# Two 1x1 products of a two-layer attention kernel: from 128 stationary columns at once to two halves of 64

## Chip, cores and metric

The kernel runs on one core of a Trainium2 chip. The metric is the device time of one execution in microseconds (us); lower is better. Times are the median of three runs where nothing else is said. A profile is one further execution, recorded by the hardware profiler.

## The reference, cut to what matters

The input x has 8 images of 256 channels and 96 x 96 pixels, in float32. Two layers follow one another, each with a group norm ahead of it and the input added after it.

```python
# layer 0: attention between channels of the 2-D Fourier transform
q_f, k_f, v_f = (fft2(pconv(gn(x), w, b)) for w, b in ((w1, b1), (w2, b2), (w3, b3)))
attn = einsum('bhcn,bhdn->bhcd', normalize(q_f), normalize(k_f)) * temperature
attn = complex(softmax(attn.real), softmax(attn.imag))
out  = abs(ifft2(einsum('bhcd,bhdn->bhcn', attn, v_f)))
x    = x + pconv(out, w_out)                       # pconv: product over the 256 channels
# layer 1: linear attention with softplus features, over the pixels
x    = x + linear_attention(gn(x), Wq, bq, Wk, bk, Wv, bv)
```

The kernel takes no Fourier transform of the images. It uses that the attention matrix of layer 0 follows from sums over pairs of pixels, and that the inverse transform of the weighted values is a fixed mixing of x with a reversed copy of it.

## The kernel before, in words

**Stages.** For each image there are five. (1) *Gram sums*: the 256 x 256 sums over pixels of products of channels, for the even and the odd part of the image (`pair_sums`, L465, with `products`, L448; image 0 has its own form, `first_sums`, L369). (2) *Attention*: softmax and the small matrices made of it, among them `mz`, the stationary matrix of z (`attention`, L556). (3) *Rotation* of the image into the array y (`rotate`, L752). (4) *Images* (`images`, L827): z = mz x y, then e = the magnitude of z, then the projection of e by `wo`, added to x. (5) *Layer 1* (`layer1`, L932, and `output`, L1120).

**Stage 4 in detail.** The 9216 pixels are cut into 24 chunks (index i) of CH = 384. For each chunk, `apply` (L864) makes two tiles of z, c = 0 and 1, each 128 output channels by 384 pixels, as the sum of two products over k (128 input channels each), at L867. VectorE adds a table and writes e (L912), ScalarE squares (L916), GpSimd adds the two halves of e (L917), ScalarE takes the root (L918, L919). The projection (`project`, L870) of the chunk two places back follows: two tiles m of 128 x 384, each a sum over two k, at L875; VectorE adds them to x (L877) and takes the statistics for the next group norm (L296). At i = 0, 8 and 16 a third, narrow kind of z is made for eight chunks at once ("z16", 32 output channels for each, four of them side by side in the array, also at L867); VectorE reads it at L897. z tiles lie in the PSUM pool `ps` (5 buffers), projection tiles in `acc` (3 buffers) or `ps`.

**Gram sums in detail.** `turn_blocks(u)` (L484) transposes 32 x 32 blocks of the next image on VectorE (L503) and, for every second u, sends the result to DRAM for later use (the transfer xtd, L508) and issues the load of a later group (`load_grouped`, L137, with its DMAs at L153 and L155). `pair(u)` (L512) makes the even and the odd part, eo, on GpSimd (L518, L530) and on GpSimd or VectorE (L531). `products` (L448) then multiplies eo with itself, in one step for each of up to three q: 8 products with 64 stationary columns, which go to the upper and the lower 64 partitions of a PSUM tile by turns (m % 2), at L462. There are 37 steps for an image after the first. eo and e share a ring of five SBUF buffers.

**What sets the order.** The order on each engine is written out by hand: it is the program order within `manual_schedule` (L1202). The stages are Python generators, and `weave` (L1111) advances the Gram sums of the next image by as many steps as a stage yields. `images` yields 1 after chunk 15 (the preparation of Gram's first pair), 2.5 after each of the chunks 16 to 23 (L924), and 1 before each of the two last projections; `layer1` yields too. So from chunk 16 on TensorE gets z, projection, then two or three Gram steps, and so on. Before chunk 16, and in the last image (which has no next one), z and projection follow each other alone. All DMAs are issued from SyncE's queue (SP).

**The lines touched.** `columns` (L743) gives the stationary columns of z:

```python
        return t[:, k, c * P:(c + 1) * P] if c < 2 else t[:, k, 2 * P:2 * P + 32]
```

A step of Gram sums uses half of the columns of the array in each product:

```python
                o = acc[c][m % 2 * HP:m % 2 * HP + HP, to:to + n]
                nc.tensor.matmul(o, lhsT=v[:, 1 + m * HP:1 + (m + 1) * HP], rhs=of, ...)
```

Here P = 128 and HP = 64.

Of the kernel before, what the change touches and what calls it, by code (L numbers as in the profile page):

```python
# [57 lines left out]
P = 128  # L58
HP = 64
KC = 2  # L60
# [14 lines left out]
def two_layer_kernel(ctx: ExitStack, tc: tile.TileContext, x, w1t, b1, w2t, b2, w3, b3, wot, temp,  # L75
                     wqt, bq, wkt, bk, wvt, bv, gavg, gmat, tmat, out):
    nc = tc.nc
# [4 lines left out]
    CH = 384  # L82
    PR = CH // W
# [33 lines left out]
    def ring_tile(name):  # L117
        return ring.tile([P, 2 * NQ * (C + 2)], F32, tag="ring", name=name)

    def ps_tile(name):  # L120
        return psum.tile([P, 512], F32, tag="ps", name=name)

    def load_x(b, t):
        nc.sync.dma_start(out=x_of(b)[:, :, t * TW:(t + 1) * TW], in_=x_v[b, :, :, t * TW:(t + 1) * TW])
# [12 lines left out]
    def load_grouped(b, v):  # L137

        xs = x[b].rearrange("(c i) h w -> i c h w", i=32)
        if 2 * v == NG:  # L140
            m = H // 2
            f, g = (staged(b, v, i)[:, 0:C].rearrange("p (c w) -> p c w", c=NB8) for i in range(2))
            for q in range(NQ):
                s = slice(32 * q, 32 * q + 32)
                n = 32 if q else 31
                o = W + 1 - 32 * (q + 1)
                nc.sync.dma_start(out=f[s], in_=xs[:, :, m, s])
                nc.sync.dma_start(out=g[s, :, 0:n], in_=xs[:, :, m, o:o + n])
            return
        f, g = (staged(b, v, i)[:, 0:SG].rearrange("p (c w) -> p c w", c=NB8) for i in range(2))  # L150
        for a in range(G):
            h, s = 2 * (G * v + a), slice(32 * a, 32 * a + 32)
            nc.sync.dma_start(out=f[s], in_=xs[:, :, h:h + 2].rearrange("p c r w -> p c (r w)"))  # L153
            if h:
                nc.sync.dma_start(out=g[s], in_=xs[:, :, H - h - 1:H - h + 1].rearrange("p c r w -> p c (r w)"))  # L155
            else:
                nc.sync.dma_start(out=g[s, :, 0:W], in_=xs[:, :, H - 1])
                nc.sync.dma_start(out=g[s, :, W:2 * W], in_=xs[:, :, 0])
# [39 lines left out]
    wo = const.tile([P, KC, C], F32, name="wo")  # L198
# [96 lines left out]
    def stats_chunk(st, b, c, k):  # L295
        nc.vector.bn_stats(out=st[:, k, c, :], in_=x_of(b)[:, k, c * CH:(c + 1) * CH])  # L296
# [4 lines left out]
    def aggregate(mv, st, k):  # L301
        nc.vector.bn_aggr(out=mv[:, k, :], in_=st[:, k, :, :].rearrange("p n s -> p (n s)"))  # L302
# [440 lines left out]
    def columns(t, k, c, j):  # L743

        return t[:, k, c * P:(c + 1) * P] if c < 2 else t[:, k, 2 * P:2 * P + 32]

    def blocks(c):
        return [slice(0, P)] if c < 2 else [slice(32 * j, 32 * j + 32) for j in range(4)]
# [78 lines left out]
    def images(b):  # L827
        mz, nmean, beta = m0.pop(b)
# [5 lines left out]
        for c in range(3):  # L834
            for j, r in enumerate(blocks(c)):
                for k in range(KC):
                    nc.tensor.matmul(pg[r, c * (H + 1):(c + 1) * (H + 1)], lhsT=columns(mz, k, c, j), rhs=ys[:, k, :],
                                          start=(c == 0 and k == 0), stop=(k == KC - 1), skip_group_check=True)
# [22 lines left out]
        st1 = new_stats(f"st1_{b}")  # L861
        mv = two.tile([P, KC, 2], F32, tag="mv", name=f"mv_b{b}")

        def apply(out, k, c, j, i):  # L864

            f, o = divmod(PR * i, HB)
            nc.tensor.matmul(out[:, 0:CH].rearrange("p (h q) -> p h q", q=PR), lhsT=columns(mz, k, c, j),  # L867
                             rhs=yz[:, k, f, :, o:o + PR], start=(k == 0), stop=(k == KC - 1), skip_group_check=True)

        def project(i, e):  # L870
            n = slice(i * CH, (i + 1) * CH)
            for m in range(KC):
                po = (ps_tile if m and b + 1 < B and i >= WI - 1 else acc_tile)(f"po_{b}_{i}_{m}")
                for k in range(KC):
                    nc.tensor.matmul(po[:, 0:CH], lhsT=wo[:, k, m * P:(m + 1) * P], rhs=e[:, k, :],  # L875
                                     start=(k == 0), stop=(k == KC - 1))
                nc.vector.tensor_add(x[:, m, n], x[:, m, n], po[:, 0:CH])  # L877
                if i == NC - 1:
                    stats_chunk(st1, b, i, m)
                    aggregate(mv, st1, m)  # L880
            if i < NC - 1:
                for m in range(KC):
                    stats_chunk(st1, b, i, m)

        pending = []
        for i in range(NC):
            if i % 8 == 0:
                v16 = []
                p16 = [ps_tile(f"z16_{b}_{i + t}") for t in (0, 4)]
                for t in range(2):  # L890
                    for k in range(KC):
                        for j, r in enumerate(blocks(2)):
                            apply(p16[t][r], k, 2, j, i + 4 * t + j)
                for t in range(2):
                    v = two.tile([P, CH], F32, tag="v16", name=f"v16_{b}_{i + 4 * t}")
                    v3 = v.rearrange("p (q h) -> p q h", h=H)
                    nc.vector.tensor_add(v3, p16[t][:, 0:CH].rearrange("p (h q) -> p q h", h=H),  # L897
                                         tab16.unsqueeze(1).to_broadcast([P, PR, H]))
                    nc.scalar.activation(v, v, AF.Square)
                    nc.gpsimd.tensor_add(v3, v3, sg[2].unsqueeze(1).to_broadcast([P, PR, H]))  # L900
                    v16.append(v)
            if i % 2 == 0 and 3 + i // 2 < NT:
                for t in range(0 if i == 0 else 3 + i // 2, 4 + i // 2):
                    load_x(b, t)
            if b + 1 < B and i in (12, 13):
                load_grouped(b + 1, i - 12)
            e = ring_tile(f"e_{b}_{i}")[:, 0:4 * CH].rearrange("p (t n) -> p t n", t=4)
            for c in range(2):
                pz = ps_tile(f"z_{b}_{i}_{c}")
                for k in range(KC):  # L910
                    apply(pz, k, c, 0, i)
                nc.vector.tensor_add(  # L912
                    e[:, 2 * c:2 * c + 2, :].rearrange("p t (q h) -> p t q h", h=H),
                    pz[:, 0:CH].rearrange("p (h q) -> p q h", h=H).unsqueeze(1).to_broadcast([P, 2, PR, H]),
                    tab[c].unsqueeze(2).to_broadcast([P, 2, PR, H]))
            nc.scalar.activation(e, e, AF.Square)  # L916
            nc.gpsimd.tensor_add(e[:, 0:2, :], e[:, 0:2, :], e[:, 2:4, :])  # L917
            nc.scalar.activation(e[:, 0:2, :], e[:, 0:2, :], AF.Sqrt)  # L918
            nc.scalar.activation(e[0:NH, 1, :], v16[i % 8 // 4][32 * (i % 4):32 * (i % 4) + NH, :], AF.Sqrt)  # L919
            pending.append((i, e))  # L920
            if len(pending) > 2:
                project(*pending.pop(0))
            if i >= WI:
                yield 2.5 if i > WI else 1  # L924
        for p in pending:
            yield 1
            project(*p)
# [274 lines left out]
    with tc.manual_schedule(engines={E.PE, E.DVE, E.Pool, E.SP, E.Activation}):  # L1202
        sums, loads, parts = first_sums(), first_loads(), tables()
        fetch, turns = rotate(0)
        next(loads)
        next(parts)
        next(loads)
        next(parts)
        next(loads)
        next(parts)  # L1210
        finish(loads)
        for i, _ in enumerate(sums):
            if i > 9:
                next(parts, None)
            if i > 14:
                next(turns)
        finish(mix(0, attention(0), turns))
        for b in range(B):
            sums = pair_sums(b + 1) if b + 1 < B else iter(())
            weave(images(b), sums)  # L1220
            weave(layer1(b), sums)
            if b + 1 < B:
                fetch, turns = rotate(b + 1)
                mixed = mix(b + 1, attention(b + 1), turns)
                output(b, *l1.pop(b), fetch, sums, mixed)
                finish(mixed)
            else:
                output(b, *l1.pop(b))
# [50 lines left out]
```

## Time and profile before

| what | value |
|---|---|
| median of three runs | 2517.08 us (2514.93 to 2518.08) |
| profiled execution, its own time | 2517.73 us |
| its span, first to last instruction | 2515.9 us, 47,106 instructions |
| mean granted TensorE clock | 0.991 |
| L867, z, 128 columns wide: passes, mean of one | 1536, 491 ns |
| L867, z16, 32 columns wide: passes, mean of one | 768, 488 ns |
| L875, projection, 128 columns wide: passes, mean of one | 1536, 488 ns |
| L462, Gram sums, 64 columns wide: passes | 4928 |
| chunks 16 to 23 of one image (849 to 926 us): busy PE, DVE, ACT, POOL | 76.62, 63.53, 23.79, 40.87 us of 77.00 |

How to read it: PE is TensorE's matmul part and PEld its loading of stationary columns; DVE is VectorE, ACT ScalarE, POOL GpSimd, SP the queue that issues DMAs. A group is named by its line, engine, operation and tile, as "L867 PE MATMUL z<-arena,mz 128*128 128x384": z is written from arena (here y) and mz, with 128 rows by 128 columns of the array in use and a moving operand of 128 x 384. A float32 product is recorded as two passes, each with a load of its own; the counts are of passes. Matmuls are pipelined and their ends are modelled, so the mean of one is longer than the distance from one start to the next. "A <- B" in a wait means that A's engine was idle until B; "<- issue" means that the profile shows nothing that was waited for.

### The profile page before, as it was taken

The numbers are of one execution on the slowest core, as the hardware profiler recorded it, in microseconds if no ns is written. First come the engines' busy times: TensorE is split into PE (matmuls) and PEld (weight loads), VectorE is DVE, ScalarE is ACT, GpSimd is POOL, SyncE is SP. The second block draws the span as 40 slices with busy tenths as digits, with TensorE's granted clock in tenths as the row PEclk, the third lists the DMA queues.
The fourth block names the chain that finished last, engine by engine and source line by source line (L and its number), as shares of the span: only waits on it lengthen the run. The fifth ranks groups of instructions, "written<-read, shape, count | busy, mean of one in ns | idle before, by whom it ended". The sixth has DMA issues, their size and how long they took to land. (4 is left out here: it accounts for less than half of the span.)

```text
span 2515.9 us, 47106 instructions
## 1 busy us (share of the span) xinstructions
PE 2475.3 (98%) x18448; PEld 1694.3 (67%) x18448; DVE 1783.9 (71%) x3472; ACT 1164.4 (46%) x2053; POOL 860.4 (34%) x820
## 2 busy tenths in 40 slices
PE   9999999999999999999999999999999999999998
PEld 7875667656686667856668566685666756677546
DVE  4467876687866878578775787757876578866776
ACT  3345364443545445354443535435363453634553
POOL 4124513245123442144331452413524136142311
PEclk9999999999999999999999999999999999999997
DMA  7134729356292653916559263683638627296004
GB/s 229 37 129 100 179 73 324 136 133 179 82 329 91 163 149 123 336 58 161 136 183 318 47 170 96 236 264 63 167 83 295 205 63 198 52 326 200 1 7 151
DMA packets 264665, 394.40 MB, mean 157 GB/s; under 512 B 37400, under 2 KB 194300, under 8 KB 264444
## 3 DMA queue, kind: packets, MB, share of 16 engines
q1 hardware_dynamic: 264444, 391.38, 52.7%
q8 instruction: 147, 2.41, 0.4%
q14 instruction: 74, 0.61, 0.1%
HBM read 246.99 MB, written 144.32 MB: 156 GB/s over the span
## 5 line engine op out<-in xcount | busy, mean ns | idle before, releaser
L867 PE MATMUL z<-arena,mz 128*128 128x384 f32 (+1 forms) x2304 | 596.9, 490 | 0.0
L917 POOL TENSOR_TENSOR e<-e 128x768 f32<-128x768 f32 x192 | 348.6, 1815 | 547.7 <-ACT e L916 521.5
L875 PE MATMUL po<-e,wo 128*128 128x384 f32 x1536 | 529.0, 488 | 1.7 <-ACT e L918 1.7
L867 PEld LDWEIGHTS z<-arena,mz 128*128 128x128 f32 (+1 forms) x2304 | 309.9, 163 | 243.2 <-issue 57.8
L875 PEld LDWEIGHTS po<-e,wo 128*128 128x128 f32 x1536 | 289.9, 190 | 207.1 <-ACT e L918 7.2
L912 DVE TENSOR_TENSOR e<-z,xT 128x768 f32<-128x768 f32 x384 | 360.9, 949 | 61.1 <-PE z L867 59.4
L806 PEld LDWEIGHTS y<-tm,arena 96*128 96x128 f32 x3072 | 360.4, 192 | 36.6 <-issue 24.8
L462 PE MATMUL acc<-eo 128*64 128x193 f32 (+6 forms) x4928 | 381.2, 305 | 0.0
L462 PEld LDWEIGHTS acc<-eo 128*64 128x64 f32 (+1 forms) x4928 | 311.3, 136 | 102.7 <-issue 75.5
L806 PE MATMUL y<-tm,arena 96*128 96x128 f32 x3072 | 380.3, 278 | 0.0
L916 ACT ACTIVATE e<-e 128x1536 f32<-128x1536 f32 x192 | 284.4, 1481 | 166.6 <-DVE e L912 164.3
L918 ACT ACTIVATE e<-e 128x768 f32<-128x768 f32 x192 | 161.9, 843 | 382.0 <-POOL e L917 378.1
L877 DVE TENSOR_TENSOR arena<-arena,po 128x384 f32<-128x384 f32 x384 | 209.1, 550 | 175.1 <-PE po L875 173.8
L530 POOL TENSOR_TENSOR eo<-arena 128x768 f32<-128x768 f32 x77 | 157.3, 2043 | 408.4 <-DVE arena L503 309.2
L1172 POOL TENSOR_TENSOR arena<-arena,po 128x384 f32<-128x384 f32 x180 | 178.6, 1011 | 207.8 <-ACT po L1171 202.4
L812 DVE COPY arena<-y 128x384 f32<-128x384 f32 (+1 forms) x192 | 104.5, 544 | 146.1 <-PE y L806 145.0
L812 ACT COPY arena<-y 128x384 f32<-128x384 f32 (+1 forms) x200 | 94.5, 472 | 231.9 <-PE y L806 214.0
L296 DVE BATCH_NORM_STATS2 st<-arena 128x6 f32<-128x384 f32 x384 | 195.0, 547 | 0.6
L1171 ACT COPY po<-o 128x384 f32<-128x384 f32 x180 | 78.5, 481 | 192.0 <-PE o L1163 189.0
L503 DVE STREAM_TRANSPOSE arena<-arena 128x768 f32<-128x768 f32 x168 | 155.1, 955 | 9.1 <-DMA xtd<-arena 7.2
L1032 PE MATMUL xT<-ident,arena 128*128 128x128 f32 x1152 | 144.1, 275 | 1.3 <-ACT xT L1035 1.3
L1032 PEld LDWEIGHTS xT<-ident,arena 128*128 128x128 f32 x1152 | 127.1, 141 | 19.0 <-issue 16.5
(249 smaller groups left out, 2584.0 us busy)
## 6 DMA issues: line engine op xcount, KB each, us to landing
arena<-in_x_dram SPq DMA_DIRECT2D x106, 768.0 KB
out_dram<-arena SPq DMA_DIRECT2D x192, 384.0 KB
xtd<-arena SPq DMA_DIRECT2D x42, 1536.0 KB
arena<-xtd SPq DMA_DIRECT2D x168, 384.0 KB
arena<-in_x_dram SPq DMA_DIRECT2D x329, 192.0 KB
tm<-rx SPq DMA_DIRECT2D x96, 159.0 KB
wl<-in_w1t_dram SPq DMA_DIRECT2D x8, 256.0 KB
wl<-in_w2t_dram SPq DMA_DIRECT2D x8, 256.0 KB
```

The source lines that it names most:

```text
L296: nc.vector.bn_stats(out=st[:, k, c, :], in_=x_of(b)[:, k, c * CH:(c + 1) * CH])
L462: nc.tensor.matmul(o, lhsT=v[:, 1 + m * HP:1 + (m + 1) * HP], rhs=of, start=(first and m < 2), stop=last, skip_group_check=True)
L806: nc.tensor.matmul(pu[:, o:o + P], lhsT=xt[:, s, k * P:(k + 1) * P], rhs=tm[:, n:n + P], start=True, stop=True)
L812: copy(y[:, :, :, g:g + nr, :], v.rearrange("p k r (f w) -> p k f r w", f=2))
L867: nc.tensor.matmul(out[:, 0:CH].rearrange("p (h q) -> p h q", q=PR), lhsT=columns(mz, k, c, j), rhs=yz[:, k, f, :, o:o + PR], start=(k == ...
L875: nc.tensor.matmul(po[:, 0:CH], lhsT=wo[:, k, m * P:(m + 1) * P], rhs=e[:, k, :], start=(k == 0), stop=(k == KC - 1))
L877: nc.vector.tensor_add(x[:, m, n], x[:, m, n], po[:, 0:CH])
L912: nc.vector.tensor_add(e[:, 2 * c:2 * c + 2, :].rearrange("p t (q h) -> p t q h", h=H), pz[:, 0:CH].rearrange("p (h q) -> p q h", h=H).uns ...
L916: nc.scalar.activation(e, e, AF.Square)
L917: nc.gpsimd.tensor_add(e[:, 0:2, :], e[:, 0:2, :], e[:, 2:4, :])
L1032: nc.tensor.transpose(pt[:, j * C + k * P:j * C + (k + 1) * P], x[:, k, o:o + P], ident)
L1172: nc.gpsimd.tensor_add(x[:, m, r], x[:, m, r], t)
```

## The change

Each z product with 128 stationary columns, and each product of the projection, becomes two with 64: one for output channels 0 to 63, one for 64 to 127, written to the upper and the lower 64 partitions of the same PSUM tile. The moving operand is the same for both. The halves alternate inside the loop over k. The narrow z16 products, everything on other engines, and the order of the stages stay.

```diff
--- before.py
+++ after.py
@@ -861,10 +861,12 @@
         st1 = new_stats(f"st1_{b}")
         mv = two.tile([P, KC, 2], F32, tag="mv", name=f"mv_b{b}")
 
-        def apply(out, k, c, j, i):
+        halves = [slice(HP * h, HP * h + HP) for h in range(2)]
+
+        def apply(out, k, c, j, i, h=slice(None)):
 
             f, o = divmod(PR * i, HB)
-            nc.tensor.matmul(out[:, 0:CH].rearrange("p (h q) -> p h q", q=PR), lhsT=columns(mz, k, c, j),
+            nc.tensor.matmul(out[:, 0:CH].rearrange("p (h q) -> p h q", q=PR), lhsT=columns(mz, k, c, j)[:, h],
                              rhs=yz[:, k, f, :, o:o + PR], start=(k == 0), stop=(k == KC - 1), skip_group_check=True)
 
         def project(i, e):
@@ -872,8 +874,9 @@
             for m in range(KC):
                 po = (ps_tile if m and b + 1 < B and i >= WI - 1 else acc_tile)(f"po_{b}_{i}_{m}")
                 for k in range(KC):
-                    nc.tensor.matmul(po[:, 0:CH], lhsT=wo[:, k, m * P:(m + 1) * P], rhs=e[:, k, :],
-                                     start=(k == 0), stop=(k == KC - 1))
+                    for h in halves:
+                        nc.tensor.matmul(po[h, 0:CH], lhsT=wo[:, k, m * P:(m + 1) * P][:, h], rhs=e[:, k, :],
+                                         start=(k == 0), stop=(k == KC - 1), skip_group_check=True)
                 nc.vector.tensor_add(x[:, m, n], x[:, m, n], po[:, 0:CH])
                 if i == NC - 1:
                     stats_chunk(st1, b, i, m)
@@ -908,7 +911,8 @@
             for c in range(2):
                 pz = ps_tile(f"z_{b}_{i}_{c}")
                 for k in range(KC):
-                    apply(pz, k, c, 0, i)
+                    for h in halves:
+                        apply(pz[h], k, c, 0, i, h)
                 nc.vector.tensor_add(
                     e[:, 2 * c:2 * c + 2, :].rearrange("p t (q h) -> p t q h", h=H),
                     pz[:, 0:CH].rearrange("p (h q) -> p q h", h=H).unsqueeze(1).to_broadcast([P, 2, PR, H]),
```

## The prediction, made before the changed kernel was run

> **What bounds the kernel now.** I read the page's first part, then the groups of instructions with shapes kept apart, then the waits, and last the timeline of the stretches in which the changed products run.
>
> ```profile
> PE 2475.3 (98%) x18448; PEld 1694.3 (67%) x18448; DVE 1783.9 (71%) x3472; ACT 1164.4 (46%) x2053; POOL 860.4 (34%) x820
> ...
> PEld acc L462 <- issue: 75.5, 155, 1.1
> ...
> PEld z L867 <- issue: 57.8, 226, 0.6
> ```
>
> TensorE is busy all the time and in the list of waits it waits for nobody by more than a few us; so its own time is the kernel's time. The two lines on PEld (the weight loads) are the ones that matter: loads of the Gram sums (L462) and of z (L867) come late by "issue", for which the profile shows no releaser. The timeline shows what that is. First, an image's early part, with z and projection only; then the late part, with Gram sums between them (columns: start us, length us, what, number of passes; each fp32 product is recorded as two passes).
>
> ```profile
> 775.42 2.74 PE L867 MATMUL z<-arena,mz 128*128 128x384 f32 x8
> 778.00 2.74 PE L875 MATMUL po<-e,wo 128*128 128x384 f32 x8
> ```
>
> ```profile
> 1182.88 3.51 PE L462 MATMUL acc<-eo 128*64 128x193 f32 x48
> 1186.32 2.85 PE L867 MATMUL z<-arena,mz 128*128 128x384 f32 x8
> 1189.01 2.74 PE L875 MATMUL po<-e,wo 128*128 128x384 f32 x8
> 1191.68 2.42 PE L462 MATMUL acc<-eo 128*64 128x193 f32 x32
> 1194.03 2.85 PE L867 MATMUL z<-arena,mz 128*128 128x384 f32 x8
> ```
>
> Read the starts, not the lengths (ends are modelled). Undisturbed, 8 passes take 778.00 - 775.42 = 2.58, that is 322.5 ns each. In the late part z takes 2.69 (+0.11) and the projection 2.67 (+0.09). Gram takes 3.44 for 48 passes and 2.35 for 32, so 16 passes (one step) take 1.09 to 1.10, and 3.44 - 3 x 1.095 = 0.155 is left over. A round trip from 128 columns to 64 and back thus loses 0.11 + 0.09 + 0.155 = about 0.35 us in which nothing is computed, though no operand is late.
>
> [...] 0.09 to 0.10 on each side of a Gram burst, and nothing between z and projection, which have different operands but one shape. [...] After a drain the first load has no matmul to lie under, and the trace shows it: z's first product is late by 0.11; of Gram's 0.155, some 0.10 is the drain and 0.05 the load. [...] 16 Gram passes are 8 side-by-side pairs of 193 and 130 columns, 2 x (2 x 193 + 2 x 130) = 1292 columns in 1.095 us, 1.18 columns per ns, against 384/322.5 = 1.19 for full width. Four z products of 32 columns (the z16 part) side by side also go at one quad per 0.32 to 0.33:
>
> ```profile
> 763.12 0.15 PEld L867 LDWEIGHTS z<-arena,mz 128*32 128x32 f32 x4 [0.17 <-issue]
> 763.45 0.15 PEld L867 LDWEIGHTS z<-arena,mz 128*32 128x32 f32 x4 [0.17 <-issue]
> 763.77 0.15 PEld L867 LDWEIGHTS z<-arena,mz 128*32 128x32 f32 x4 [0.17 <-issue]
> ```
>
> **The change, part by part.**
>
> *The halves themselves.* 1536 z passes and 1536 projection passes of 128 columns become 3072 pairs of 64. The order (half 0, half 1, then the next k) alternates the two column tiles as Gram's m does, so I expect pairs. Their pace is the unknown. Per pair Gram has 1.095/8 = 137 ns for a mean of 161.5 columns; [...] Bounds: below, no gain (the columns streamed are the same); above, Gram's rate per column, 384/1.18 = 325.5 ns, +3 ns x 3072 = 9.2 us. I take 0 and keep 9.2. The 3072 matmuls and 3072 loads more are 4 instructions per 322.5 ns, 12 per us; Gram runs 32 per 1.095, 29 per us, so issuing hides under the matmuls, and so do two loads of about 0.14 each. If that cover failed it would show as the slower rival below. Readers on VectorE wait for half 1's last pass, some 13 ns later: nothing.
>
> *Drains removed.* By the code, an image with Gram beside it has Gram after i = 16 to 23 (8 bursts) and after each of the two last projections: 10 entries from the projection, of which 9 return to z or projection (the tenth goes to the 128-column group norm and keeps its cost). Seven images have one. An entry loses 0.09 + 0.05 = 0.145 or so, a return 0.10 + 0.11 = 0.205. 70 x 0.145 + 63 x 0.205 = 10.2 + 12.9 = **23.1 us**.
>
> *z16 to z.* 24 switches from 32 columns to 128 become 32 to 64: the drain stays, the open load is half, 24 x 0.053 = **1.3 us**. Projection to z16 keeps its drain.
>
> *Given back at the image's ends.* The group norm after the last burst waits for the mean and variance, which follow the last projection through VectorE (the wait of gm_b for mv_b). So the last entry's 0.145 only lengthens that wait: -7 x 0.145 = -1.0. At an image's start the first projection waits for the first e, so that z16's gain is doubtful: -8 x 0.053 = -0.4. In the last image a new switch 64 to 128 falls into a wait of over 2 us: 0.
>
> *Given back at Gram's operands.* This is the term I am least sure of. TensorE comes earlier to each Gram pair u; does its operand eo? In the third image:
>
> ```profile
> 854.33 0.38 SPq L508 DMA_DIRECT2D xtd<-arena  x1
> 860.92 1.84 DVE L503 STREAM_TRANSPOSE arena<-arena 128x768 f32<-128x768 f32 x2 [0.93 <-DMA xtd<-arena]
> 868.01 2.59 POOL L530 TENSOR_TENSOR eo<-arena 128x768 f32<-128x768 f32 x1
> 870.30 2.42 PE L462 MATMUL acc<-eo 128*64 128x193 f32 x32
> 877.69 1.84 POOL L531 TENSOR_TENSOR eo<-arena 128x768 f32<-128x768 f32 x1
> 878.01 3.51 PE L462 MATMUL acc<-eo 128*64 128x193 f32 x48
> ```
>
> Pair 2 is ready at 868.01 + 2.59 = 870.60 and used at the second step of its burst, 870.30 + 0.05 + 1.10 = 871.45: 0.85 to spare. Pair 3 is ready at 879.53 and used at the third step, 878.01 + 0.05 + 2.20 = 880.26: 0.73 to spare (in the other six images the same rows give 0.45 to 0.77, mean 0.66). From 846 to 874 VectorE runs without waiting for TensorE (transposes, then a wait for the xtd transfer, then e, which GpSimd needs before it starts on eo). So these two times don't move with TensorE. Before pair 3, TensorE will have saved 0.05 + 4 x 0.145 + 3 x 0.205 = 1.25. It therefore waits for 1.25 - 0.66 = 0.59, plus some 0.10 to start again (0.05 from an ACT end to the load it releases, as for the first projection of an image, and the open load of 0.05): 0.69 x 7 = **-4.8 us**. From both sides: 0, if the chain moves along after all; -1.25 x 7 = -8.8 if nothing is to spare. Later pairs have 1.45 and more to spare, with VectorE paced by z again.
>
> **The sum**, against the profiled execution's 2517.73 (span 2515.9 and 1.8 around it): 23.1 + 1.3 - 1.0 - 0.4 - 4.8 = 18.2 us less, 2499.5. That execution is 0.65 above the median of 2517.08, so for the median **2499.0 us** (0.7% less).
>
> **Rivals.**
>
> *A, slower: the two halves don't start together.* In the z16 rows four loads of 0.11 are spread over 0.15, 13 ns from one to the next. If every pair paid such a stagger in the array, 3072 x 13 = 40 us come on top: 2499 + 40 = 2539. For it: two tiles reading the very same moving columns at once is what Gram, with different columns, doesn't show. Against: quads and Gram pairs keep the full pace in spite of their stagger. It decides from 18.2/3072 = 5.9 ns per pair on, and beyond 7.6 ns the kernel is slower by 0.2%.
>
> *B, no change: the gap isn't the tiling.* It could be the semaphore on z's first load, or the change of shape of the moving operand. Then it stays, and the time is 2517, give or take 3. Against: Gram's first load after the projection waits for no semaphore and loses as much; projection after z waits for one and loses nothing.
>
> *C, a smaller gain: pairs at Gram's pace per column (+9.2), or Gram starved by its operands beyond what I took (-4 more):* 2503 to 2511, middle 2508.
>
> **How the numbers follow.** Forecast 0.80, around 2499; its own range goes from 2493 (no give-back at the operands: 2517.1 - 23.0 = 2494, and one more for the spread of the runs, 2514.9 to 2518.1) to 2504. C 0.08, B 0.05, A 0.07. The range of 8 in 10 reaches into C: 2493 to 2508. A difference of under 0.2% (5 us) can't be told from none; forecast and C are faster than that: faster 0.88, same 0.05, slower 0.07.
>
> **What would show it.** Right: z and projection in pairs, 16 passes per 2.58 us in the early part; in the late part 2.58 too, and Gram steps at 1.095 with no rest; PEld's "issue" before L462 and L867 falling from 75.5 and 57.8 to a small part (the z16 switches remain); a new wait of TensorE on POOL eo of some 0.6 us once per image, seven times. Wrong: 16 passes over 2.60 us (A or C), drains that remain at the bursts' edges (B), or waits for eo of over a us. The likeliest error is in the give-back, which is worth up to 5 us either way.

## The result, and the profile after

| | before | after |
|---|---|---|
| median of four runs each | 2516.01 us (2513.68 to 2518.08) | 2494.79 us (2492.63 to 2495.90) |
| ratio, with its 95% interval | | 0.9915 (0.9898 to 0.9932) |
| profiled execution, its span | 2517.73, 2515.9 us | 2492.63, 2490.8 us |

The changed kernel is 21.2 us (0.85%) faster; the prediction said 2499.0, 18.2 us faster. In the lines of the kernel after, z is L869, the projection L878, its add to x L880, the add on VectorE that makes e L916, the sum of e's halves on GpSimd L921; L462, L503, L530 and L531 have kept their numbers. First the busy times, then the lines of the list of waits that answer to those shown of before.

```profile
PE 2446.4 (98%) x21520; PEld 1573.5 (63%) x21520; DVE 1785.9 (72%) x3472; ACT 1163.7 (47%) x2053; POOL 861.9 (35%) x820
```

```profile
PEld z L869 <- issue: 289.4, 1534, 0.6
PEld po L878 <- issue: 237.2, 1353, 0.2
PEld acc L462 <- issue: 54.8, 192, 1.1
...
PEld acc L462 <- POOL eo L530: 1.4, 5, 0.4
```

TensorE still sets the time. PE's busy time fell by 29 us although its passes rose from 18448 to 21520. "issue" ahead of z did not fall but rose fivefold; the last line, a wait for GpSimd's eo, is new and small. Both are taken up below. Now the timeline: the early part of an image, and the late part of the third image with Gram sums between (start us, length us, what, passes).

```profile
772.95 2.75 PE L869 MATMUL z<-arena,mz 128*64 128x384 f32 x16
775.53 2.75 PE L878 MATMUL po<-e,wo 128*64 128x384 f32 x16
```

```profile
853.34 3.47 PE L462 MATMUL acc<-eo 128*64 128x193 f32 x48
856.63 2.76 PE L869 MATMUL z<-arena,mz 128*64 128x384 f32 x16
859.21 2.76 PE L878 MATMUL po<-e,wo 128*64 128x384 f32 x16
861.79 2.48 PE L462 MATMUL acc<-eo 128*64 128x193 f32 x32
```

Twice the passes of half the width take what the full ones took: 775.53 - 772.95 = 2.58. In the late part z and projection now take 2.58 as well (859.21 - 856.63 and 861.79 - 859.21), where 2.69 and 2.67 stood. A burst of 48 Gram passes takes 856.63 - 853.34 = 3.29 = 3 x 1.097 and leaves no rest. After the burst of 32 the next z starts at 864.09; so it takes 2.30, 0.11 more than two steps: that is a wait for pair 2 (kernel 11 below makes it go away).

A single number sums this up for each kernel: the length of the stage, from an image's first pass for the tables that are added to z (tile zs) to the first pass of its group norm (tile gm_b). In the third image that is 760.41 to 925.15 before and 752.88 to 914.33 after: 164.74 and 161.45. The mean over the seven images with Gram sums beside them goes from 164.75 to 161.56, 3.19 each; the last image, which has none, from 137.75 to 137.47. Together 7 x 3.19 + 0.28 = 22.6 us, which accounts for the 21.2 between the medians. The rest of an image (gm_b to the next zs) takes 140.1 to 140.3 in both kernels, but for 0.3 more behind the sixth image in both, and for 1.57 more in some places (twice before, once after); what that is stands at the end. The two profiled executions differ by more than the medians do, 25.1 us in their spans. The 2.5 that are left lie outside the stage: one place of 1.57 less, 0.1 more in each of the seven gaps between images, 1.8 less behind the last group norm and 0.3 more ahead of the first image. Except for the 0.1 per gap, which all kernels with a projection in halves or quarters show, nothing ties them to the change.

### The profile page after: what moved, and what is told of

Same layout as the page of the kernel before. It is cut to its first block, busy times and chain, and to the rows that moved or that the text cites. A ratio compares the mean times of both kernels' runs of the same rounds, so it can differ in the third digit from the quotient of the medians.

```text
span 2490.8 us, 53254 instructions
## 1 busy us (share of the span) xinstructions
PE 2446.4 (98%) x21520; PEld 1573.5 (63%) x21520; DVE 1785.9 (72%) x3472; ACT 1163.7 (47%) x2053; POOL 861.9 (35%) x820
## 5 line engine op out<-in xcount | busy, mean ns | idle before, releaser
L869 PE MATMUL z<-arena,mz 128*64 128x384 f32 (+1 forms) x3840 | 592.4, 487 | 0.0
L921 POOL TENSOR_TENSOR e<-e 128x768 f32<-128x768 f32 x192 | 349.5, 1820 | 533.1 <-ACT e L920 507.1
L878 PE MATMUL po<-e,wo 128*64 128x384 f32 x3072 | 529.5, 486 | 1.8 <-ACT e L922 1.8
L869 PEld LDWEIGHTS z<-arena,mz 128*64 128x64 f32 (+1 forms) x3840 | 245.4, 131 | 296.0 <-issue 289.4
L878 PEld LDWEIGHTS po<-e,wo 128*64 128x64 f32 x3072 | 227.9, 137 | 266.3 <-issue 237.2
L916 DVE TENSOR_TENSOR e<-z,xT 128x768 f32<-128x768 f32 x384 | 358.9, 947 | 43.4 <-PE z L869 42.6
L462 PE MATMUL acc<-eo 128*64 128x193 f32 (+6 forms) x4928 | 379.1, 303 | 1.1 <-DVE eo L417 0.9
L462 PEld LDWEIGHTS acc<-eo 128*64 128x64 f32 (+1 forms) x4928 | 326.5, 136 | 82.0 <-issue 54.8
L880 DVE TENSOR_TENSOR arena<-arena,po 128x384 f32<-128x384 f32 x384 | 208.2, 550 | 153.8 <-PE po L878 153.5
L530 POOL TENSOR_TENSOR eo<-arena 128x768 f32<-128x768 f32 x77 | 157.6, 2047 | 399.7 <-DVE arena L503 309.1
L503 DVE STREAM_TRANSPOSE arena<-arena 128x768 f32<-128x768 f32 x168 | 155.0, 954 | 23.3 <-DMA xtd<-arena 20.5
```

Of the source, the lines that this page charges most:

```text
L878: nc.tensor.matmul(po[h, 0:CH], lhsT=wo[:, k, m * P:(m + 1) * P][:, h], rhs=e[:, k, :], start=(k == 0), stop=(k == KC - 1), skip_group_che ...
L916: nc.vector.tensor_add(e[:, 2 * c:2 * c + 2, :].rearrange("p t (q h) -> p t q h", h=H), pz[:, 0:CH].rearrange("p (h q) -> p q h", h=H).uns ...
```

## The experiments

**Theory.** What went is the loss at each change between 128 and 64 columns; the halves themselves cost nothing; and the Gram sums' operands give back part of it. **Rivals.** The gain comes from something else in the narrower products (one product alone would bring part of it); the pairs have a price that other savings hide; the give-back at the operands is large or nil. No kernel here leaves out or changes any of the computation: edits split products, or move them. "Stage" is the length just defined, and times "against before" are against the kernel before on the same chip (2516.18, one run, for kernels 1 to 4, 2516.81 for 5 to 8, 2514.76 for 9 to 12). Kernels without an interval had one profiled run; such a total can be off by a few us, so the argument rests on the stage and on rows.

### 1. Only z in halves

The projection goes back to one product of 128 columns.

```diff
-                    for h in halves:
-                        nc.tensor.matmul(po[h, 0:CH], lhsT=wo[:, k, m * P:(m + 1) * P][:, h], rhs=e[:, k, :],
-                                         start=(k == 0), stop=(k == KC - 1), skip_group_check=True)
+                    nc.tensor.matmul(po[:, 0:CH], lhsT=wo[:, k, m * P:(m + 1) * P], rhs=e[:, k, :],
+                                     start=(k == 0), stop=(k == KC - 1))
```

> Halves for z alone, the projection in one piece of 128 columns. Theory (what was saved is the switch of tiling, 0.145 us from 128 to 64 columns and 0.205 back): now every chunk has both switches. Per image with Gram beside it, against the kernel before: 22 switches z to projection (+4.5), 12 back to z (+1.7), 7 returns from Gram to z saved (-1.4), z16 to z (-0.2): +4.7 us; last image +7.1. In all +40 us: 2556 against 2516. Rival (the halves save something of their own, or the gap belongs to the Gram operands and not to the tiling): each half of the change brings its share, so 2505 to 2510.

Measured: 2553.99, 38 us slower than before; the stage is longer than before's by 4.46 per image with Gram (4.7 worked out) and by 6.7 in the last one (7.1). Its timeline, in the early part where no Gram sums run (the projection is L877 in this kernel):

```profile
781.37 2.85 PE L877 MATMUL po<-e,wo 128*128 128x384 f32 x8 [0.18 <-ACT e L921]
784.14 2.80 PE L869 MATMUL z<-arena,mz 128*64 128x384 f32 x16
786.88 2.85 PE L877 MATMUL po<-e,wo 128*128 128x384 f32 x8
```

z in halves takes 786.88 - 784.14 = 2.74 and the projection at full width 784.14 - 781.37 = 2.77, where 2.58 stood for each of them as long as both had one shape. Two switches per chunk cost 0.35, the sum that before lost around a Gram burst. So the narrow z brings nothing by itself (the projection alone in halves was not run); what counts is that neighbours have the same tiling. Both products here have moving operands of 384 columns, so a change of the moving operand's shape is not what costs.

### 2 and 3. More boundaries, before and after

Each burst of 2.5 Gram steps is cut in two of 1.25, one of them put between z and the projection of a chunk. That doubles the boundaries and leaves the work alone.

```diff
             pending.append((i, e))
+            if i > WI:
+                yield 1.25
             if len(pending) > 2:
                 project(*pending.pop(0))
             if i >= WI:
-                yield 2.5 if i > WI else 1
+                yield 1.25 if i > WI else 1
```

On the kernel before:

> The kernel before, with each of the bursts of Gram steps after chunks 16 to 23 cut in two, one between z and projection and one after the projection; the steps are the same in number. Theory: 8 more round trips in each of 7 images at 0.35 us, 56 x 0.35 = 19.6 us more: 2536 against 2516. Rival (the gaps come from operands or semaphores that are late, which a finer mixture would rather relieve): no change or a little faster, 2510 to 2517.

Measured: 2548.01; 4.75 per image on the stage where 2.8 was worked out for the switches. On the kernel after:

> The changed kernel, with the same finer mixture as the run before it. Theory: in one tiling a boundary costs nothing, so twice as many of them cost nothing: 2495, give or take 2. Rival (part of the cost of a boundary is still there): up to 20 us more.

Measured: 2528.21, 33 us off. The waits of this second kernel (us in all, times, longest):

```profile
PEld acc L462 <- POOL eo L530: 14.8, 7, 2.1
...
PEld acc L462 <- POOL eo L518: 8.7, 7, 1.2
```

The new boundaries cost nothing: in the third image a projection starts at 857.20, 16 Gram passes at 859.78 and z at 860.88, which is 2.58 and 1.10. But the first half of each burst now runs earlier than in the old order, by a projection, and reaches pairs that aren't ready: 14.8 and 8.7 us, and 4.8 for an eo of VectorE (L527), are 28.3 us of waits. Kernel 2 waits for L518 and L527 too, 4.8 and 4.2 us, which is part of why it missed its own number (its stages are 7 x (4.75 - 2.8) = 13.7 us over it). The edit had thus moved work as well as boundaries, and a cleaner one was needed.

### 9 and 10. The same, with no Gram step earlier than it was

The half bursts are put later instead: the first chunk of the series passes one over, and the last half follows the loop.

```diff
             pending.append((i, e))
+            if i > WI + 1:
+                yield 1.25
             if len(pending) > 2:
                 project(*pending.pop(0))
             if i >= WI:
-                yield 2.5 if i > WI else 1
+                yield 1.25 if i > WI else 1
+        yield 1.25
         for p in pending:
```

On the kernel before:

> The kernel before, with the bursts of Gram steps cut in two once more, but so that half of a burst comes later than it did (between the z and the projection of the next chunk) instead of half of it earlier, since the earlier halves ran into operands that were not ready. Theory: 7 more round trips in each of 7 images at 0.35 us, 17 us more: 2533 against 2516, and 2.45 us more per image in the stage of z and projection. Rival (the cost seen in the first pair of such runs was the finer mixture itself, not the switch): as much as in the changed kernel with the same mixture.

Measured: 2533.93, and 2.52 per image on the stage, as worked out (2.45). Its rows:

```profile
862.86 2.85 PE L875 MATMUL po<-e,wo 128*128 128x384 f32 x8
865.63 1.32 PE L462 MATMUL acc<-eo 128*64 128x193 f32 x16
866.88 2.85 PE L867 MATMUL z<-arena,mz 128*128 128x384 f32 x8
869.66 2.42 PE L462 MATMUL acc<-eo 128*64 128x193 f32 x32
```

Now each of three neighbours pays at its start or end: projection 2.77 for 2.58, one Gram step 1.25 for 1.095, z 2.78 for 2.58. A round trip added, 0.35 us added. On the kernel after:

> The changed kernel with that same later mixture. Theory: nothing per boundary, and the pairs of operands have a little more time, so 2494 to 2495.5 and the stage unchanged or 0.1 to 0.2 us shorter per image. Rival: as much more as the kernel before with this mixture has, 10 to 17 us.

Measured: 2520.81, again a miss, by 26 us. Its rows:

```profile
861.00 2.75 PE L878 MATMUL po<-e,wo 128*64 128x384 f32 x16
863.58 1.27 PE L462 MATMUL acc<-eo 128*64 128x193 f32 x16
864.67 2.75 PE L869 MATMUL z<-arena,mz 128*64 128x384 f32 x16
867.25 2.37 PE L462 MATMUL acc<-eo 128*64 128x193 f32 x32
...
876.54 1.32 PE L462 MATMUL acc<-eo 128*64 128x193 f32 x16 [0.66 <-POOL eo L530]
```

The first four rows are the theory at its plainest: 2.58, 1.09, 2.58, 2.19 for two steps, with a boundary at each. (Gram's two steps end where the next projection starts, at 869.44.) The last row is what made it slow. GpSimd and VectorE prepare the next pair while TensorE works off z and projection; with the burst cut in two, the wait for a pair falls into a place where TensorE has nothing in hand, and the waits for L530 and L531 sum to 22 us. In the kernel before, the time lost in switches was cover for that chain of preparations: with the same mixture kernel 9 has 0.2 us of waits for L531 and none for L530. So this pair shows the price of a boundary in rows, in both kernels, but not in the total of the second.

### 4. The odd part first

The prediction had Gram's operand due at a step's start. In `products` the loop over c takes the even half of eo first (made by L530) and the odd half (L531, made after it) second. This kernel turns that round.

```diff
     def products(acc, eo, q, np_, first, last):
-        for c in range(2):
+        for c in (1, 0):
```

> The changed kernel, with the loop over the even and the odd part inside one Gram step turned round: the odd part first. My theory for the smaller give-back: a step uses the even part in its first half and the odd part only 0.55 us later, and what is late at pair 3 is the odd part (the subtraction comes after the addition on GpSimd), so that the forecast put its need half a step too early. With the odd part first the forecast's wait is there: about 0.38 + 0.1 us at pair 3 of each image, 7 x 0.45 = 3 us more, 2498 against 2495, and the stage of z and projection 0.4 us longer per image. Rival (the chain that makes the operands moved along with TensorE): no change in that stage.

Measured: on the stage 0.40 per image, as expected; on the total 2505.67, 7.7 more than expected. The stage first. In the changed kernel the third image's pair 3 is made like this:

```profile
868.21 1.83 POOL L530 TENSOR_TENSOR eo<-arena 128x768 f32<-128x768 f32 x1
869.99 1.83 POOL L531 TENSOR_TENSOR eo<-arena 128x768 f32<-128x768 f32 x1
```

and used like this:

```profile
869.25 3.47 PE L462 MATMUL acc<-eo 128*64 128x193 f32 x48
```

The third step begins at 869.25 + 2.19 = 871.44. The even half, ready at 868.21 + 1.83 = 870.04, is long there; the odd half, ready at 871.82, is not, but is needed only half a step later, at 871.99: 0.17 to spare, no wait. With the odd half first:

```profile
872.32 2.38 PE L462 MATMUL acc<-eo 128*64 128x193 f32 x32
...
875.11 1.32 PE L462 MATMUL acc<-eo 128*64 128x193 f32 x16 [0.40 <-POOL eo L531]
```

The step that should start at 872.32 + 2.19 = 874.51 starts at 875.11, 0.60 late, when the odd half (ready at 875.05 here) is there: close to the give-back that the prediction had worked out (0.69). The stage is only 0.40 longer because the wait for pair 2 is gone at the same time: its even half is now needed half a step later, and the burst in which pair 2 starts takes 2.19 in each image. So the reckoning for pair 3 was right, and the order within the step was what it left out. The other 7.7 us of the total lie outside the stage; see the last section.

### 5. Halves outside the loop over k

```diff
-                for k in range(KC):
-                    for h in halves:
+                for h in halves:
+                    for k in range(KC):
```

(for z and for the projection.) The program order is now four passes on the lower tile, then four on the upper.

> The changed kernel, with the loop over the halves outside the one over k: four passes in a row go to one column tile, then four to the other. Theory (TensorE takes work for a free column tile from several instructions ahead, as it must already do for the two passes of one product): still pairs, 2495 give or take 2. Rival (products start in program order, and only neighbours in that order pair up): the second half starts with the last pass of the first, 6 pass times for what took 4, up to half as much again on the 990 us of z and projection: up to 2980.

Measured: 2502.15, 7 us off, though the pairs are there. Rows in the early part:

```profile
773.34 0.49 PE L878 MATMUL po<-e,wo 128*64 128x384 f32 x1
773.58 0.49 PE L869 MATMUL z<-arena,mz 128*64 128x384 f32 x1
...
775.92 0.49 PE L869 MATMUL z<-arena,mz 128*64 128x384 f32 x1
```

The projection's first pass (773.34) starts ahead of z's last (773.58): each tile runs through its own passes, the upper one 0.24 us behind, and a projection still takes 2.58, up to the next z's first pass (775.92 - 773.34). So the pairing doesn't hang on strict alternation. The stage is 0.62 per image longer than the changed kernel's. Set side by side in the third image, the rows of the two kernels differ by 0.60 up to the z16 products of chunk 8, by 0.05 more up to those of chunk 16, and by nothing at the Gram bursts, apart from pair 2: the lag comes to light ahead of a switch to another tiling, and Gram has the same one. The last image loses 1.2, half of it (0.57) from its last three projections to the group norm. Kernel 5 is 9.5 us longer than the changed kernel's profiled execution (2492.63): 7 x 0.62 + 1.2 = 5.5 in the stage, and 3 x 1.57 = 4.7 in three more of the places that the last section describes.

### 6. Quarters of 32

```diff
-        halves = [slice(HP * h, HP * h + HP) for h in range(2)]
+        halves = [slice(32 * h, 32 * h + 32) for h in range(4)]
```

This gives z and projection the tiling of the z16 products; against Gram (64) the tilings still differ.

> Four quarters of 32 columns in place of two halves, for z and projection in all chunks: the tiling of z16, not that of Gram. Theory: switches to and from Gram are back, at 0.148 into Gram and 0.122 out of it (drain 0.095, open load 0.053 or 0.027), those at z16 are gone. Against the kernel before per image: 9 x 0.083 + 3 x 0.20 + 2 x 0.12 = 1.6 us less, 8 images 12 us: 2504. Rival (four tiles that read the same moving columns, or four times the instructions, cost pace): 8 quads take more than 2.58 us, and each percent of that is 10 us: over 2510.

Measured: 2504.17, and on the stage 1.41 per image less than before (1.6 worked out), 0.92 less in the last one (0.84).

Four tiles that read the same moving columns also keep the pace: in the early part the 32 passes of a z start at 772.47 and the projection at 775.05, 2.58 later. What remains against the changed kernel is the loss at the switches around Gram sums, now with loads of 32 columns. Beside Gram, z now takes 2.60 and the projection 2.69: what z pays after a switch is 0.02 with 32 columns, where it was 0.11 with 128, while the projection's 0.11 ahead of one is about what it was (0.09). The traces of before and after show two parts of this, pass by pass. From the last pass of 384 columns ahead of a switch to the first one behind it is 0.416 us from start to start (0.322 within a run), whether the new passes have 32, 64 or 128 stationary columns. And the first pass behind it lasts 0.510, 0.537 or 0.590 us in turn, where 0.486 is usual: 0.024, 0.051 and 0.104 more (ends are modelled, but at 128 columns the next start is later by as much, 0.427 behind the first and not 0.322). Each width lost where its neighbour had another one.

### 7 and 8. Quarters where no Gram sums run, halves beside them

`parts_at(i)` returns quarters for the chunks up to 15 and for the whole last image, halves otherwise; the loops over h go through it. The changed kernel ran beside it again.

```diff
-        halves = [slice(HP * h, HP * h + HP) for h in range(2)]
+        parts = [[slice(n * h, n * h + n) for h in range(P // n)] for n in (32, HP)]
+        def parts_at(i):
+            return parts[1 if b + 1 < B and i > WI else 0]
```

> Quarters where z and projection lie between z16 products only (chunks up to 15, and the whole last image), halves where they lie between Gram steps. Theory: of the switches that the changed kernel keeps, those at z16 go, two to three per image at 0.12 to 0.15 us, 0.39 us in each of 7 images and 0.5 in the last, 3 us, with 1 us more that is doubtful at the first chunk: 2491.5 against 2495, the fastest. Rival (quarters lose pace): slower than the changed kernel.

> The changed kernel unaltered, on the same chip as the one with quarters then halves, for the comparison of the two: 2495, and 21 us less than the kernel before.

Measured: 2493.41 (2491.88 to 2494.59), ratio to before 0.9907 (0.9890 to 0.9923), and for the changed kernel 2495.71 (2494.31 to 2496.79), ratio 0.9918 (0.9903 to 0.9933). The intervals overlap. On the stage it gains only 0.5 us over all eight images, all of it in the last one (0.64): the losses at z16 are gone in the other seven too, but TensorE reaches pair 2 sooner and waits there (for L530 5.4 us in seven images, 1.6 in kernel 8).

### 11 and 12. Pair 2 made earlier

GpSimd makes pair 2 in the order of the program, where its work is given out together with pair 1's first step. Here it is put ahead, right behind the transposes that it needs; 12 is the same with 7's quarters.

```diff
                     prepare(("turn", u + 2), lambda u=u: turn_blocks(u + 2))
+                    if b and u == 0:
+                        prepare(("pair", 2), lambda: make(2))
```

> The changed kernel, with the preparation of Gram pair 2 put right after the transposes that feed it, ahead of the next chunk's e on GpSimd and VectorE. Theory: the start of pair 2 is where TensorE waits once per image in the changed kernel (about 0.1 to 0.3 us with the restart, 7 images); ready some 3 us sooner, that wait goes, and pair 3's transposes come sooner too: 1 to 2 us less, 2494 against 2495.5, the stage 0.15 to 0.25 us shorter per image. Rival (it is not the chain through GpSimd that makes pair 2 late): no change.

Measured: 2491.57 (2490.91 to 2494.14), ratio 0.9910 (0.9895 to 0.9924); the stage 0.18 per image shorter than in kernel 8. That is 1.3 of the 4.1 us between the medians of the two, whose intervals overlap and which ran on different chips. GpSimd and TensorE in it:

```profile
854.62 2.61 POOL L530 TENSOR_TENSOR eo<-arena 128x768 f32<-128x768 f32 x1 [1.09 <-DVE arena L503]
```

```profile
861.14 2.38 PE L462 MATMUL acc<-eo 128*64 128x193 f32 x32
```

Pair 2 is ready at 854.62 + 2.61 = 857.23 and due at 861.14 + 1.10 = 862.24, 5.0 to spare; the next z starts at 863.33, so the burst takes 2.19 instead of 2.30, and the list of waits has no line of L462 for L530 any more.

> Quarters then halves, with pair 2 prepared early. In the run of quarters then halves TensorE reached pair 2 half a us sooner in each image and lost all of it waiting there. Theory: with pair 2 ready the half us stays: 7 x 0.7 + 0.6 = 5.5 us less than the changed kernel, 2490, the fastest of all. Rival (the next pair binds at once): 2493, as without the early preparation.

Measured: 2488.69 (2486.71 to 2490.28), ratio 0.9895 (0.9878 to 0.9911), the fastest of all; the stage 0.67 per image shorter than kernel 8's (0.7 worked out) and 0.62 in the last image (0.6). The saving at z16 that kernel 7 had waited away is there once the operand is. Its runs all lie below those of kernel 11, on the same chip (2490.91 to 2494.14), and below those of the changed kernel; but the runs of kernel 8 are from another chip, and the intervals of their ratios to before overlap.

## Why the prediction was right, and where it was not

**The mechanism and the pairs' pace** (taken at 0, which was the author's estimate, with 9.2 kept): right. 2.58 us for 16 passes as for 8; rival A's stagger does not appear, and with C's upper pace a product would have taken 2.60. Kernel 1 rules out B: no Gram operand is near, the moving operands have one shape, and a difference in width between neighbours costs 0.35 us per round trip. Kernels 9 and 10 say the same from the other side: one mixture, the same operands with the same moving shapes, and the 0.35 is there in the one and absent in the other.

**Losses at the switches removed** (0.145 per entry, 0.205 per return): right, and a little small. What the prediction calls a drain is a later start, by 0.09 us in the traces; whether TensorE empties there, no view shows. Its open load answers to the longer first pass: behind a return z's lasts 0.590 us instead of 0.486, behind an entry Gram's 0.378 instead of 0.327 (before, 1186.32 and 1191.68), 0.104 and 0.051 more. Per image the prediction's terms are 10 x 0.145 + 9 x 0.205 = 3.30, plus z16's 0.16, minus 0.145 and 0.05 at the ends: 3.26. Kernel 11, in which no operand is waited for there, is 164.75 - 161.38 = 3.37 below before. Of the 0.11 more, 0.07 is there by the first Gram burst, which comes 0.27 sooner after the stage's start than before, where the terms give 0.20; the nine round trips take 0.353 each, against 0.350.

**z16 and the image's ends**: small, and a little too small. The last image, in which only z16's term stands, gained 0.28, where 3 x 0.053 less 0.05 gives 0.11. (The 0.053 is there: the first z pass behind z16 lasts 0.590 us before and 0.537 after.) Its two later z16 parts, each up to the next projection, take 5.35 instead of 5.40, as forecast; the first projection takes 2.63 instead of 2.69, and from the last three projections to the group norm it is 11.04 instead of 11.14. Nothing was forecast for these last two, and why they are shorter was not traced.

**Given back at Gram's operands** (-4.8): this is the term that was mis-sized. Pair 2's 0.85 us to spare was read rightly, but nothing was taken for it, although the prediction's own savings up to there, 0.05 + 3 x 0.145 + 2 x 0.205 = 0.90, use that up: TensorE now comes about when pair 2 is ready, and the burst in which it starts takes 0.06 to 0.37 longer than two steps. Pair 3, which made the whole term, was read wrongly: the step was taken to need all of eo at its start, while the half that comes last is needed 0.55 later. That is the 0.60 of kernel 4, which vanishes in the order that the kernel has. In place of 0.69 x 7 = 4.8 the give-back is pair 2's 0.18 x 7 = 1.3 (kernel 11 against kernel 8). With it the prediction's sum is 23.1 + 1.3 - 1.0 - 0.4 - 1.3 = 21.7 us, against 22.6 in the stage (0.7 of it lost again in the gaps between images) and 21.2 between the medians. The total alone could not have shown this: the interval of the ratio is 17 to 26 us less, and holds 18.2 as well as 21.7.

**The signs that it named.** 16 passes per 2.58, in both parts, and Gram steps without a rest: found. "A new wait of some 0.6 us once per image on POOL eo": not found; 1.4 us in five waits stand in its place. "PEld's issue falling": this was a wrong sign. The line of the Gram loads in the third image's late part (846 us to the group norm before, 836 us after), before and then after:

```profile
PEld acc L462 <- issue: 5.5, 10, 0.5
```

```profile
PEld acc L462 <- issue: 2.7, 16, 0.2
```

Gram's ten waits of 0.55, one per entry, are gone, and those that remain are 0.17 long. But 0.17 is what a pair of loads of 64 columns leaves under a pass of 384 columns:

```profile
857.92 0.16 PEld L869 LDWEIGHTS z<-arena,mz 128*64 128x64 f32 x2 [0.17 <-issue]
```

Such rows follow each other every 0.32 us: two loads take 0.16 of it, the loading part rests for the other half, and that is counted as "issue" before z and the projection, 1534 and 1353 times, at no cost. In the stages that follow in the same image, where Gram bursts stand beside products of other shapes, the L462 line is the same before and after (4.6 us, nine times): those losses remain. Some 7 x 4.6 = 32 of the 75.5 us were thus never the change's to save, which the sign left out as well.

## What to carry to other kernels

Where a busy TensorE changes between products of unlike tilings, read the starts of undisturbed runs and of those at the boundary: the difference (here 0.35 us per round trip) went here when the wide products were cut to the narrow ones' width, and the cutting cost nothing, as the parts ran side by side (2.58 us for 8 or 16 passes). Then look at what the lost time had covered: take each operand's time at the instruction that reads it, not at the start of the step, and look whether its maker can be put earlier, as pair 2's could. Cutting only one of two neighbours was worse than cutting none (kernel 1, 38 us).

## What the runs showed of the hardware that was not expected

**Windows at half the clock.** Kernel 4's total was 7.7 us above what was expected, though its stage was as expected. The table by window (us, busy PE, PEld, DVE, ACT and POOL, granted clock, DMA share, GB/s) shows where, in the stage in which layer 1 is written out:

```profile
987.00:989.00 2.00, 2.00 (x19) 1.38 (x16) 0.55 (x1) 0.86 (x2) 0.87 (x1) 0.69 0.97 294
989.00:991.00 2.00, 2.00 (x14) 0.65 (x10) 0.00 (x0) 0.00 (x0) 1.08 (x2) 0.50 1.06 394
991.00:993.00 2.00, 2.00 (x28) 1.33 (x24) 1.02 (x2) 0.86 (x2) 1.15 (x2) 0.96 1.08 286
```

The granted clock is 0.69, 0.50 and 0.96 in turn, and it was 1.00 in each window at this place in the changed kernel: 0.31 x 2 + 0.50 x 2 + 0.04 x 2 = 1.70 us of lost clock: one stretch of some 3.4 us at half speed. (TensorE waited 0.42 us at 985.7, some 2 us ahead of it, and was busy for the other 2.99 of the 3.41 us up to it, 984.35 to 987.76; but the changed kernel has the same wait.) Gram's 16 passes take 989.47 - 987.42 = 2.05 there, where the changed kernel's take 984.96 - 983.71 = 1.25. An image with such a stretch is 1.57 us longer; kernel 4 has seven, before two, the changed kernel one, kernel 11 none. Of the 13.0 us by which kernel 4's profiled execution is longer than the changed kernel's, 2.8 are in the stage, 6 x 1.57 = 9.4 in these stretches and 0.8 elsewhere.

The starts of the stretches tell more. In kernel 4 they lie at 380.19, 683.98, 987.77 us and so on, 303.79 apart, which is 89 x 3.4133; in the changed kernel at 1587.96, 2403.74, 2454.94 and 2482.25, which is 239, 15 and 8 such steps apart; in the kernel before at 688.22, 1910.19, 2425.61 and 2483.63, 358, 151 and 17 steps apart (from 2400 on all of them lie behind the last image's stage). So in each of these executions they keep to a grid of 3.413 us. An image of kernel 4, its stretch included, takes 303.8 us, so that the same work meets the grid at the same place in every image; an image of the changed kernel takes 301.8, which is 88.4 of these steps, and the place moves on. That would explain seven against one, but no run tested it, and what in the work sets a stretch off stays open. One stretch more or less moves a total by some 1.6 us (1.57 above).

**Tiles out of step.** Kernel 5: with four passes for one column tile, then four for the other, both kept the full pace, one 0.24 us behind the other. Kernels 6 and after: two or four tiles that read the same moving columns cost nothing against one (2.58 us for 8, 16 or 32 passes).
